# One 128-column matmul where both halves of a block list a chunk

## The chip, the cores and the metric

The kernel runs on one core of a Trainium2 chip. The metric is the device time of one execution in microseconds; the kernel before took 2024.06 us as the median of 7 runs (2017.86 to 2031.18). The engines are named as in the profile: PE is TensorE (PEld its weight loads), DVE is VectorE, ACT is ScalarE, POOL is GpSimd, and SP is the engine that only issues transfers.

## The reference

Two graph layers over 4096 nodes with 512 features. The adjacency matrix is sparse, some 32 neighbours a node, and given as a dense 4096 x 4096 array. Each layer normalizes its input first and adds its result to it.

```
h = max(layernorm(x), 0)
x = x + relu((d * adj * d^T) @ h @ W + b)            # layer 0
h = max(layernorm(x), 0)
e = leaky_relu(Wh1 + Wh2^T, 0.2)                     # layer 1, on h
att =  softmax(where(adj > 0,  e, -1e12))
neg = -softmax(where(adj > 0, -e, -1e12))
x = x + elu(concat(att @ h, neg @ h) @ wtrans)
```

## The kernel before

Layer 0 is computed densely on TensorE from the start to about 960 us. Beside it the kernel works out, for every pair of 64-row blocks of layer 1, which nodes its rows have as neighbours, sorted into lists of 128 places ("chunks"), so that layer 1 need not touch the rest.

Layer 1 (`sparse_layer1`) treats 64 blocks of 64 rows. Two blocks, numbered r = 2n and 2n + 1, form a pair n and share their gathered rows. For a pair POOL issues 21 indirect DMAs (`gather`, L506), one a chunk of 128 rows of 644 words, into three tiles: g0 with 8 chunks, g1 with 6 and a seventh that SP loads, the block's own rows, and g2 with 7. The even block r = 2n multiplies the chunks of g0 and g1, 15 of them, and the odd block those of g1 and g2, 14 of them. Each of the three tiles has two buffers, used by alternate pairs, so that the gathers of a pair can begin when the pair two places earlier has been read: those into g0 after its even product, those into g1 and g2 after its odd one. POOL runs them in this order: 8 gathers into g0, then 13 into g1 and g2, then 8 again. Which matmul they wait for is the last one that reads the tile's buffer.

A block's 64 rows are two halves of 32 rows. Each row has two weights for a neighbour, one for each softmax. The weights of a chunk are thus a tile of 128 columns, `p[:, k]`, ordered half, softmax, row: 64 columns for the first half and 64 for the second. A half does not have neighbours in every chunk. `HALVES` says which chunks each half needs, 10 of 15 in an even block and 11 of 14 in an odd one. `half_products` (L551) goes through both lists side by side: each step is two matmuls with 64 weight columns each, one writing rows 0 to 63 of the accumulator u and one writing rows 64 to 127, with different gathered rows streaming through each. An even block has 10 such steps, an odd one 11. In f32 each matmul appears as two weight loads and two matmul records.

The lists overlap. In even blocks both halves need chunks 3, 4, 10, 11 and 14, in odd ones 0, 1, 2, 3, 4, 6, 9 and 10. The kernel before multiplies these twice, once for each half, in different steps.

After a product (`product`, with the sums of the weights, cs, L580) ACT scales u into us (L1815). PE transposes us one block later (tp, L595), ACT copies the transposed values, and PE multiplies them by `wtrans` into o (`project1`, L1826): eight 128-column matmul records after every block. DVE and ACT finish o (L1843 to L1847) and SP stores it. The weights of the block two ahead (`weights`, L1765 to L1787) are made by ACT and DVE meanwhile. The order of instructions on each engine in layer 1 is set by a scheduler from the program's order; matmuls that are marked keep their place.

The loop over the blocks runs in this order for block k (abridged):

```
product(r)
if k + 4 - k % 2 < len(order):
    for a in ((0,), (1, 2))[k % 2]:
        gather1(order[k + 4 - k % 2] // 2, a)
if k + 2 < len(order):
    weights(order[k + 2])
if k:
    turn(order[k - 1])
```

The first pair is treated earlier (`product0`, L1541 for its sums), and two blocks have two more chunks that are multiplied apart (`late_h`).

Of the kernel before, what the change touches and what calls it, by code (L numbers as in the profile page):

```python
# [32 lines left out]
RB = 64  # L33
# [15 lines left out]
HALVES = (  # L49
    ((0, 1, 2, 3, 4, 10, 11, 12, 13, 14), (3, 4, 5, 6, 7, 8, 9, 10, 11, 14)),  # L50
    ((0, 1, 2, 3, 4, 6, 9, 10, 11, 12, 13), tuple(range(11))),
)
# [221 lines left out]
def gcn_gat_kernel(  # L274
# [26 lines left out]
    nc = tc.nc  # L301
# [36 lines left out]
    with sbuf(name="init", bufs=1) as init:  # L338
        column = init.tile([P, P], F32, name="column")
        nc.vector.memset(column[:, 0:1], 0.0)  # L340
        n = 1
# [60 lines left out]
    steps = [(c, r) for c in range(NK) for r in range(CAPS[c] // 8)]  # L402
# [148 lines left out]
    def half_products(r, u, p, row, chunks, end=True, pin=False, begin=True):  # L551


        for ks in zip(*chunks):
            for h, k in enumerate(ks):
                i = nc.tensor.matmul(  # L556
                    u[h * RB : (h + 1) * RB],
                    p[:, k, h].rearrange("p g i -> p (g i)"),
                    row(k),
                    start=begin and k == HALVES[r % 2][h][0],  # L560
                    stop=end and k == chunks[h][-1],
                )
                if pin:
                    tc.keep_in_program_order(i)

# [41 lines left out]
    with sbuf(name="y0", bufs=1) as y_pool, sbuf(name="wa", bufs=1) as wa_pool, sbuf(name="bits", bufs=4) as bits_pool, sbuf(name="small0", bufs=4) as small, ExitStack() as rest, ExitStack() as lists:  # L607
# [5 lines left out]
        def list_tables(pool):  # L613
            rank = pool.tile([P, EN], F32, name="rank")
            nc.gpsimd.iota(
                rank,
                [[-1, EN]],
                base=EN,
                channel_multiplier=0,
                allow_small_or_imprecise_dtypes=True,  # L620
            )
            before = pool.tile([P, NE + 1, NH], F32, name="before")
            start = pool.tile([NH, 1], F32, name="start")
            nc.gpsimd.iota(
                start,
                [[0, 1]],
                base=0,
                channel_multiplier=STR,
                allow_small_or_imprecise_dtypes=True,
            )  # L630
            return rank, before, start

        rank, before, start = list_tables(list_pool)
# [400 lines left out]
        def new_rows(pool, n):  # L1034
            rows = [pool.tile([P, ROW_W], F32, tag=f"h{k}", name=f"h{k}", bufs=1) for k in range(n)]
            for h in rows:
                nc.gpsimd.memset(h[:, ROW_T + 1 :], 0.0)
            return rows
# [94 lines left out]
        i0, n = GROUPS[0]  # L1133
# [362 lines left out]
        def early_pair(work, at_pool, prod, rows):  # L1496
# [63 lines left out]
            def product0(r):  # L1560
                u0[r] = bank(f"u{r}")

                def row(k):
                    gt, k0, n = parts0(r)[k >= parts0(r)[1][1]]
                    return gt[:, k - k0, :F].bitcast(F32)

                half_products(r, u0[r], ps0[r], row, HALVES[r % 2], False, r == blocks[0])

            def late_product0(r):
                def row(k):  # L1570
                    return late_h[:, k - slots0(r), :F]

                late = range(slots0(r), slots0(r) + n_late)
                half_products(r, u0[r], ps0[r], row, (late, late), begin=False)
                sum0(r, late)
# [77 lines left out]
        with sbuf(name="work0", bufs=2) as work, sbuf(name="rows0", bufs=1) as row_pool, sbuf(name="sums", bufs=3) as sum_pool, sbuf(name="at", bufs=6) as at_pool:  # L1653
# [4 lines left out]
            with tc.manual_schedule(engines=order - {engine.PE}):  # L1658
                rows = new_rows(row_pool, 3)
# [31 lines left out]
    def sparse_layer1():  # L1691
        nonlocal verdict
        with ExitStack() as pools:
# [105 lines left out]
            def product(r):  # L1799
                p, total = wgt.pop(r)  # L1800

                rl = None if r in first else inverse_sums(small, r, total)
                u = bank(f"u{r}")

                def row(k):
                    gt, k0, n = parts(r)[k >= parts(r)[1][1]]
                    return gt[:, k - k0, :F].bitcast(F32)

                half_products(r, u, p, row, HALVES[r % 2], r not in with_late)
                if r in with_late:  # L1810
                    ks = range(n_late)
                    half_products(r, u, lates.pop(r), lambda k: late_h[:, k, :F], (ks, ks), begin=False)
                rl = rl or inverse_sums(small, r, total)
                us[r] = work.tile([P, F], F32, tag="us", name=f"us{r}")
                nc.scalar.activation(us[r], u, AF.Copy, scale=rl)  # L1815
# [169 lines left out]
```

## Time and profile before

| what | us |
|---|---|
| median of 7 runs | 2024.06 |
| the profiled execution | 2027.42 |
| its span, first to last instruction | 2025.6 |
| PE busy | 1896.8 |
| L556 (u), 64-column matmul records x2604, busy | 624.4 |
| idle of PE just before L556 | 88.2 |
| L1826 (o), 128-column matmul records x496, busy | 230.9 |
| POOL gathers L506 x672, busy | 639.1 |
| mean granted TensorE clock | 0.974 |

The profiled execution lies 3.4 us above the median. Busy times of PE count overlapping records once. "Issue" as the cause of idle time means that the engine waited for nothing that the profile shows; "remote" means that a semaphore was raised by something that the profile can't name.

### The profile page before, as it was taken

The page shows a single profiled execution, that of the slowest core. Times are in us where ns is not written, and L with a number is a line of the kernel's source. Part 1 is how long each engine was busy: PE and PEld are TensorE (multiplying, and loading weights), DVE is VectorE, ACT ScalarE, POOL GpSimd, SP SyncE. Part 2 cuts the span into 40 slices and gives each one's busy share as a digit, 9 for nine tenths or more (in the row PEclk, how much of TensorE's full clock was granted, in tenths as well). Part 3 has the DMA queues.
Part 4 walks back from the last instruction along what each step waited for, and adds up shares of the span by engine and source line. Part 5 has one row for each costly group of instructions (what it writes and reads, how often), then busy time and mean ns, then how long its engine had stood idle before and what let it go on. Part 6 is the DMA issues. An engine that isn't in the chain of part 4 may idle for free.

```text
span 2025.6 us, 24509 instructions
## 1 busy us (share of the span) xinstructions
PE 1896.8 (94%) x7708; PEld 1056.3 (52%) x7708; DVE 1273.9 (63%) x2758; ACT 937.4 (46%) x2165; POOL 822.0 (41%) x919
## 2 busy tenths in 40 slices
PE   8999999999999999999779999999889898898988
PEld 3444468888888888884333333333333333333334
DVE  6766588898889979752625654646545555554552
ACT  6777733222213212221536654646555565564551
POOL 3110000033322233305536656666666666666640
PEclk9999999999999999999779989999999999998999
DMA  9999957576857676668857878788888787777850
GB/s 373 392 329 337 321 192 250 176 244 200 274 169 258 196 234 216 213 201 287 288 183 247 283 234 292 251 282 254 278 263 298 248 251 249 249 257 232 254 180 23
DMA packets 217218, 504.33 MB, mean 249 GB/s; under 512 B 35059, under 2 KB 69395, under 8 KB 217078
## 3 DMA queue, kind: packets, MB, share of 16 engines
q0 software_dynamic: 62560, 233.71, 35.8%
q1 hardware_dynamic: 114240, 236.49, 34.5%
q10 hardware_dynamic: 40278, 32.47, 5.1%
q8 instruction: 63, 1.03, 0.2%
q14 instruction: 77, 0.63, 0.1%
HBM read 457.77 MB, written 103.45 MB: 277 GB/s over the span
## 4 chain that ended last, share of the span: by engine, by line
PE 86%; issue 6%; DVE 2%; POOL 2%; ACT 1%; another core or an unknown queue 1%; DMA 1%; DVEq 0%; POOLq 0%; ACTq 0%
PE p L1105 30%; PE u L556 28%; PE o L1826 10%; PE acc L1064 5%; PE yp L890 5%; PE q L1465 3%; PE tp L595 2%; POOL g L506 2%; PE counts L867 1%; PE cs L1541 1%; PE tx L831 1%; DMA g<-table,idx 1%; DVE total L1787 0%; ACT z L1765 0%
## 5 line engine op out<-in xcount | busy, mean ns | idle before, releaser
L506 POOL DMA_INDIRECT g<-table,idx x672 | 639.1, 951 | 441.7 <-issue 176.1
L556 PE MATMUL u<-g,p 128*64 128x512 f32 x2604 | 624.4, 606 | 88.2 <-issue 76.7
L556 PEld LDWEIGHTS u<-g,p 128*64 128x64 f32 x2604 | 190.2, 138 | 460.5 <-issue 441.1
L442 POOL DMA_INDIRECT ld<-lst,off x160 | 144.0, 900 | 342.9 <-DMA ld<-lst,off 143.4
L1765 ACT ACTIVATE z<-s,g 128x64 f32<-128x64 f32 x812 | 259.5, 320 | 46.9 <-DMA g<-table 12.5
L1105 PE MATMUL p<-y,at 128*128 128x256 f32 x832 | 248.0, 380 | 0.7 <-issue 0.7
L1105 PE MATMUL p<-y,sums 128*128 128x256 f32 x832 | 247.4, 379 | 0.0
L1105 PE MATMUL p<-t,sums 128*128 128x256 f32 x832 | 245.3, 379 | 0.0
L1826 PE MATMUL o<-wt,ut 128*128 128x512 f32 x496 | 230.9, 610 | 1.8 <-DVE eo L1843 1.4
L1768 DVE TENSOR_TENSOR z<-z,y 128x512 f32<-128x512 f32 (+1 forms) x124 | 80.3, 648 | 209.7 <-ACT y L1767 109.1
L1787 DVE TENSOR_REDUCE total<-p 128x128 f32<-128x1920 f32 (+1 forms) x62 | 207.8, 3352 | 2.1
L1105 PEld LDWEIGHTS p<-y,at 128*128 128x128 f32 x832 | 157.1, 190 | 24.1 <-issue 3.2
L1105 PEld LDWEIGHTS p<-t,sums 128*128 128x128 f32 x832 | 158.0, 190 | 21.7 <-issue 0.2
L1105 PEld LDWEIGHTS p<-y,sums 128*128 128x128 f32 x832 | 158.0, 190 | 21.4
L1826 PEld LDWEIGHTS o<-wt,ut 128*128 128x128 f32 x496 | 93.4, 199 | 96.3 <-issue 94.6
L1777 DVE SCALAR_TENSOR_TENSOR p<-g,z 128x512 f32<-128x512 uint8 (+1 forms) x124 | 78.4, 632 | 103.1 <-ACT z L1773 86.5
L852 ACT ACTIVATE junk<-ar 128x1024 bf16<-128x1024 f32 x128 | 134.5, 1051 | 9.6 <-DMA ar<-in_adj 5.6
L930 ACT ACTIVATE m<-at 128x1024 uint8<-128x1024 f32 x110 | 113.0, 1047 | 53.4 <-DVE t_all L1032 14.4
L1773 ACT ACTIVATE e<-z 128x512 f32<-128x512 f32 (+1 forms) x124 | 67.1, 542 | 132.2 <-issue 79.2
L1777 DVE SCALAR_TENSOR_TENSOR p<-g,e 128x512 f32<-128x512 uint8 (+1 forms) x124 | 79.0, 637 | 74.3 <-ACT e L1773 26.0
L1105 PE MATMUL p<-t,at 128*128 128x256 f32 x416 | 123.9, 380 | 1.2 <-DVE w L975 1.2
L1064 PE MATMUL acc<-y,at 128*128 128x512 f32 x256 | 120.2, 594 | 0.0
(220 smaller groups left out, 2032.2 us busy)
## 6 DMA issues: line engine op xcount, KB each, us to landing
ar<-in_adj SPq DMA_DIRECT2D x128, 512.0 KB
at<-in_adj_t SPq DMA_DIRECT2D x112, 512.0 KB
table<-table SPq DMA_DIRECT2D x49, 1032.0 KB
table<-m ACTq DMA_DIRECT2D x48, 256.0 KB
g<-table,idx POOLq DMA_INDIRECT x672
g<-table SPq DMA_DIRECT2D x32, 322.0 KB
at<-in_adj_t SPq DMA_DIRECT2D x32, 256.0 KB
xr<-in_x SPq DMA_DIRECT2D x32, 256.0 KB
```

The costliest lines, as they stand in the source:

```text
L442: return nc.gpsimd.indirect_dma_start(out=lst_dram[g][e % TURNS][:, :], out_offset=bass.IndirectOffsetOnAxis(ap=off[g][:, e, c : c + 1], a ...
L506: i = nc.gpsimd.indirect_dma_start(out=gt[:, k, :], out_offset=None, in_=table[2 * n // RPT], in_offset=bass.IndirectOffsetOnAxis(ap=idx[n ...
L556: i = nc.tensor.matmul(u[h * RB : (h + 1) * RB], p[:, k, h].rearrange("p g i -> p (g i)"), row(k), start=begin and k == HALVES[r % 2][h][0 ...
L852: nc.scalar.activation(junk, ar, AF.Identity, accum_out=parts[j][:, c : c + 1])
L890: nc.tensor.matmul(yp, hx_t[j][:, c * P : (c + 1) * P], w0_sb[:, c, :], start=c == 0, stop=c == FC - 1,)
L930: nc.scalar.activation(m, at, AF.Sign)
L1064: nc.tensor.matmul(a, at[:, 0, it * P : (it + 1) * P], y0[j], start=j == 0, stop=j == NJ - 1)
L1105: i = nc.tensor.matmul(out, left[:, x * P : (x + 1) * P], right, start=jp == 0 and first, stop=jp == NP - 1 and (final or not first),)
L1765: nc.scalar.activation(z[:, c], s, AF.Identity, bias=t[:, c])
L1777: nc.vector.scalar_tensor_tensor(p[:, k : k + n, :, g], mask.rearrange(four, h=2), 0.0, x.rearrange(four, h=2), ALU.is_gt, ALU.mult,)
L1787: nc.vector.tensor_reduce(total, q, AX.X, ALU.add)
L1826: i = nc.tensor.matmul(halves[j], uts[j][:, g, c, :], wts[g][:, c, :], start=g == 0 and c == 0, stop=g == 1 and c == FC - 1,)
```

## The change

In `half_products`, chunks that stand in both halves' lists are taken out of the lists. They are multiplied first, each by one matmul with all 128 columns of `p[:, k]`, into all 128 rows of u. What is left of the two lists, five chunks a half in an even block and three in an odd one, then follows in pairs of 64 columns as before. The accumulation begins with the first step and ends with the last.

```diff
-        for ks in zip(*chunks):
-            for h, k in enumerate(ks):
-                i = nc.tensor.matmul(
-                    u[h * RB : (h + 1) * RB],
-                    p[:, k, h].rearrange("p g i -> p (g i)"),
-                    row(k),
-                    start=begin and k == HALVES[r % 2][h][0],
-                    stop=end and k == chunks[h][-1],
-                )
+        both = [k for k in chunks[0] if k in chunks[1]]
+        alone = zip(*[[k for k in ks if k not in both] for ks in chunks])
+        steps = [(k, k) for k in both] + list(alone)
+        for n, (k0, k1) in enumerate(steps):
+            start, stop = begin and n == 0, end and n + 1 == len(steps)
+            if k0 == k1:
+                halves = [(u, p[:, k0].rearrange("p h g i -> p (h g i)"), k0)]
+            else:
+                halves = [
+                    (u[h * RB : (h + 1) * RB], p[:, k, h].rearrange("p g i -> p (g i)"), k)
+                    for h, k in enumerate((k0, k1))
+                ]
+            for rows, left, k in halves:
+                i = nc.tensor.matmul(rows, left, row(k), start=start, stop=stop)
```

An even block now has the steps 3, 4, 10, 11, 14 and then (0, 5), (1, 6), (2, 7), (12, 8), (13, 9); an odd one 0, 1, 2, 3, 4, 6, 9, 10 and then (11, 5), (12, 7), (13, 8). The last step that reads g0 (chunks 0 to 7 of an even block) is the eighth where it was the fifth; the last that reads g1 in an odd block (chunks 0 to 6) is the ninth where it was the seventh. Line numbers below the function grow by 5.

## The prediction

> **What bounds the kernel now.** I read the page first, for engine shares and the chain.
>
> ```profile
> PE 1896.8 (94%) x7708; PEld 1056.3 (52%) x7708; DVE 1273.9 (63%) x2758; ACT 937.4 (46%) x2165; POOL 822.0 (41%) x919
> PE 86%; issue 6%; DVE 2%; POOL 2%; ACT 1%; another core or an unknown queue 1%; DMA 1%; DVEq 0%; POOLq 0%; ACTq 0%
> L556 PE MATMUL u<-g,p 128*64 128x512 f32 x2604 | 624.4, 606 | 88.2 <-issue 76.7
> L1826 PE MATMUL o<-wt,ut 128*128 128x512 f32 x496 | 230.9, 610 | 1.8 <-DVE eo L1843 1.4
> ```
>
> TensorE carries the chain, and the line that changes, L556, is 28% of it. But L556 also has 76.7 us of idle time put down to "issue", a wait for nothing that the profile shows, while L1826 has almost none. The list of waits says how it is spread, and that POOL has a twin of it:
>
> ```profile
> POOL g L506 <- remote: 81.5, 27, 3.2
> POOL g L506 <- PE u L556: 80.8, 25, 12.5
> PE u L556 <- issue: 76.7, 63, 3.0
> ```
>
> Then the timeline of PE and of POOL over one pair of blocks. Each f32 matmul is two records, so an odd block (11 steps) is 44 and an even one (10 steps) 40.
>
> ```profile
> 1399.36 9.66 PE L556 MATMUL u<-g,p 128*64 128x512 f32 x44
> 1408.96 0.66 PE L595 MATMUL tp<-ident,us 128*128 128x128 f32 x4
> 1409.45 3.60 PE L1826 MATMUL o<-wt,ut 128*128 128x512 f32 x8
> 1412.88 0.28 PE L580 MATMUL cs<-ones,total 128*128 128x1 f32 x2
> 1413.09 7.94 PE L556 MATMUL u<-g,p 128*64 128x512 f32 x34
> 1423.02 0.59 PE L556 MATMUL u<-g,p 128*64 128x512 f32 x1 [1.99 <-issue]
> 1424.44 2.72 PE L556 MATMUL u<-g,p 128*64 128x512 f32 x5 [0.83 <-issue]
> ...
> 1431.20 0.28 PE L580 MATMUL cs<-ones,total 128*128 128x1 f32 x2
> 1431.40 1.08 PE L556 MATMUL u<-g,p 128*64 128x512 f32 x4
> ```
>
> ```profile
> 1405.88 0.94 POOL L506 DMA_INDIRECT g<-table,idx  x1 [4.59 <-PE u L556]
> ...
> 1420.88 0.95 POOL L506 DMA_INDIRECT g<-table,idx  x1 [0.30 <-issue]
> 1424.86 0.95 POOL L506 DMA_INDIRECT g<-table,idx  x1 [3.04 <-remote]
> ```
>
> The odd product runs without a gap; the even one stops near its end, and so does nearly every even product. POOL issues 13 gathers (1405.88 to 1421.82), then waits 3.04 us. By the program's order its next gather, into g0, waits for the tenth matmul of the even product. That one ended at 1417.6 by its record, but the trace's semaphore events have its increments at 1424.558 and 1424.600. So PE's increments are held back. Over the 28 runs of 13 gathers this increment comes 18.6 to 18.9 us after the run's first gather, and increments due from about 7.2 us on come late, in steps of about 0.7 us. In the hold PE still passes 57 to 70 instructions (weight loads and matmul records; median 61.5 counted from 7.2 us; two runs 79 and 82), then one per 0.7 us until the hold ends. The median slow part lasts 4.7 us. No view names what holds them; that PE's budget is counted in instructions is my inference. Two things speak for it. Between 1001 and 1014 us L1541's matmuls, which increment nothing, crawl at the same 0.7 us. And in the pair below the even product began late, so that L1826 (4 instructions per 0.86 us, not 8) filled more of the hold:
>
> ```profile
> 1092.11 3.70 PE L1826 MATMUL o<-wt,ut 128*128 128x512 f32 x8 [1.35 <-DVE eo L1843]
> 1095.86 8.59 PE L556 MATMUL u<-g,p 128*64 128x512 f32 x37
> 1105.30 1.09 PE L556 MATMUL u<-g,p 128*64 128x512 f32 x3 [0.86 <-issue]
> ```
>
> There 37 records passed, not 34, and the slow part was 2.1 us.
>
> **The change, part by part.** *Array time.* 44 records of pairs take 9.60 us to the next line's start, 0.86 a step; eight records of L1826, four 128-column matmuls, take 3.43, also 0.86. Even blocks share 5 chunks and keep 5 pairs, odd share 8 and keep 3: 10 and 11 steps, as before. So array time is 0 changed. This is the main trap: two 64-column matmuls already run side by side. Weight loads, two of 190 ns in place of four of 138, lie under 0.43 us records: 0, with that cover everywhere.
>
> *Instructions.* A shared step has 4, not 8. Even: 80 to 60; odd: 88 to 56.
>
> *The hold, one pair, t=0 at the odd product's start.* Before: 9.60 + tp 0.49 + o 3.43 + cs 0.21 puts the even product at 13.7, and 8.6 + 4.1 more make 26.4 without idle. Starts from 1080.28 to 1680.68 hold 19 pairs, 31.6 each, so 5.2 are lost. Of these the crawl takes 4.7 minus 6 instructions' work (0.65), 4.0; half-clock stretches after it (granted clock 0.96 to 0.98) and short waits take the rest.
> After: two releases move. Gathers into g1 wait for the last odd step that reads g1: step 7 before, step 9 now. So POOL's run begins 1.7 later, 8.1 instead of 6.4; the hold is 15.3 to 26.8 instead of 13.6 to 25.1. The g0 release moves from even step 5 to step 8 (t=20.6): still inside, so the 8 gathers into g0 start at 27.1, 1.7 later. SP's load of the own chunk waits for the same g1 release; a few SP transfers swap places with it, and both are needed a pair later: 0. POOL's order, ACT's and DVE's are unchanged.
> PE in the new hold: shared steps until 18.0 (2.7 us, 13 instructions), 5 pair steps to 22.3 (40), tp to 22.8 (8): 61. Net of one leaving per 0.7 us the old budget is 61.5 - 6.9/0.7 = 52 (48 to 69), the new count at 22.8 is 50, and L1826 adds 3.2 a us: PE slows at 23.4, inside o. To 26.8 that is 3.4 us, in which 5 instructions (1.05 us of o's work) pass: 2.35 lost instead of 4.0. Gain 1.65, times 28 pairs: 46 us.
> Bounds: at 48 it slows at 22.6 and loses 4.15 - 0.9, a gain of 0.75 a pair (21 us); at 69 it never slows, and POOL is next: 13 gathers 15.95 + gap 3.03 + 8 gathers 9.69 + 0.30 = 29.0 a pair, a gain of at most 2.6 (73 us). I take 46; most counts are 48 to 58 net.
>
> *The switch inside a product.* No row shows a 512-wide 128-column matmul followed by 64-column ones. Nearest: pair to tp starts 0.52 apart where 0.43 is usual, 0.09 more; each product has two such changes before and after. Bounds: 0 (the cs switch does it already) to 0.21 (a record's 0.59 must drain, less 0.43, plus 0.05 on the first record's 643 ns). I take 0.05, near the 0.09: 62 products, 3 us. [...]
>
> *Increments.* The last four 64-column matmuls of each product now increment one by one: 6 in an even product instead of 3, 5 in an odd instead of 2. The two increments above stand 42 ns apart; 3 x 42 ns x 62 is 8 us at most, and none below, but all but the last fall under the next step: I take 0. [...]
>
> *Start of layer 1.* PE crawls in L1541 too, to 1014.6, set by POOL; fewer instructions ahead of it are worth 0 to 3 us. I take 0.
>
> *What is next.* ACT's us of the even block comes at 27 instead of 27.8, and its transposes a product later; DVE's eo already cost o 1.35 us once. I count neither.
>
> Sum: 46 - 3 = 43 less. The profiled execution took 2027.42 (span 2025.6), 3.4 above the median 2024.06 of seven (2017.86 to 2031.18): 1984, and against the median **1981**. The profiled time lies in the band of the others, so I take it that the crawl is in all of them.
>
> **Rivals.** *A, no change.* The budget is time, not instructions: PE stops 7 us after the hold begins. Then run, hold and crawl move together 1.7 later and the loss stays: 2024. For it: most crawls start at 13.4 to 15.0 of the run. Against it: the pair at 1095.
> *B, slower.* A is true and the switch inside a product costs its 0.21: 62 x 0.21 = 13, so 2037. It decides once the crawl shrinks by less than 0.46 us a pair. For it: pairs and 128-column work never follow each other at full width now. Against it: the 0.09 at tp.
> *C, POOL bound.* No crawl, 29.0 a pair: 2024 - 73 = 1951. Against it: held gathers still follow PE's release.
> That the 128-column matmuls aren't made is excluded by the program's order.
>
> **The numbers.** My forecast 0.60 (1960 to 2006), C 0.08, A 0.12, B 0.20. This kernel's times spread so that some 0.3% can be told from no change. Faster 0.68, same 0.12, slower 0.20. Range 1949 to 2032: C's end to most of B; about 0.2 is left out.
>
> **What will show it.** L556's records fall from 2604 to some 1800 (128-column 806, 64-column 992) with about 0.43 us a step record; POOL's g L506 <- remote gap stays near 3.0; its runs start later after the odd product's start; "issue" before PE moves from u to o or tp and shrinks to about 45 us; pairs of about 30.0 us. Wrong if the odd or even product grows beyond 9.6 and 8.6 us where nothing stops it, or the idle at "issue" keeps its 77 us.

## The result, and the profile after

The changed kernel takes 2003.74 us (median of 13 runs, 1990.05 to 2018.25) beside 2025.60 us for the kernel before (34 runs). The ratio is 0.9891, with a 95% interval of 0.9869 to 0.9913: 22 us or 1.1% faster. The forecast was 43 us, 1981. The direction was right and the forecast gain was twice too large.

Its profiled execution took 2014.11 us (span 2012.3, mean granted clock 0.970), 10 us above its own median, so the two profiles differ by 13 us and not by 22. From the page of the changed kernel: engine shares, chain, the groups of u and o, and below them the waits of POOL and PE.

```profile
PE 1901.9 (95%) x6860; PEld 1086.3 (54%) x6860; DVE 1273.4 (63%) x2758; ACT 937.6 (47%) x2165; POOL 822.4 (41%) x919
PE 71%; issue 9%; POOL 8%; DVE 4%; DMA 2%; another core or an unknown queue 2%; ACT 2%; POOLq 0%; DVEq 0%; ACTq 0%
L567 PE MATMUL u<-g,p 128*128 128x512 f32 (+1 forms) x1798 | 636.9, 621 | 53.9 <-issue 49.4
L1831 PE MATMUL o<-wt,ut 128*128 128x512 f32 x496 | 231.7, 609 | 10.9 <-DVE rl L590 4.4
```

```profile
POOL g L506 <- PE u L567: 79.2, 20, 9.1
POOL g L506 <- remote: 65.4, 23, 3.6
PE u L567 <- issue: 49.4, 55, 5.1
```

Idle time before u fell from 88.2 to 53.9 us (-34.3); idle time before o rose from 1.8 to 10.9 (+9.1); and u itself is busy 636.9 us instead of 624.4 (+12.5; on a chip where nothing stops PE it is +9.0, from 574.1 to 583.1). These three make -12.7 of the 13.3 us between the spans. The chain no longer stays with PE: POOL's share went from 2% to 8%. Waits of POOL's gathers for something unnamed came down from 27 to 23 although the program's runs of 8 and 13 gathers are the same: some runs no longer end where they did. The timeline shows that, first PE and then POOL, over one stretch of the changed kernel (start, length, engine, line, tiles, number of records, and in brackets the idle time before):

```profile
1291.74 0.66 PE L600 MATMUL tp<-ident,us 128*128 128x128 f32 x4
1292.23 3.60 PE L1831 MATMUL o<-wt,ut 128*128 128x512 f32 x8
1295.81 6.93 PE L567 MATMUL u<-g,p 128*128 128x512 f32 x15
1303.55 0.59 PE L567 MATMUL u<-g,p 128*128 128x512 f32 x1 [0.81 <-issue]
1304.95 0.59 PE L567 MATMUL u<-g,p 128*64 128x512 f32 x1 [0.81 <-issue]
1306.38 1.01 PE L567 MATMUL u<-g,p 128*64 128x512 f32 x1 [0.84 <-issue]
1308.51 1.01 PE L567 MATMUL u<-g,p 128*64 128x512 f32 x1 [1.11 <-issue]
1309.93 3.72 PE L567 MATMUL u<-g,p 128*64 128x512 f32 x9 [0.41 <-issue]
```

```profile
1284.35 0.95 POOL L506 DMA_INDIRECT g<-table,idx  x1 [0.30 <-issue]
1288.42 0.94 POOL L506 DMA_INDIRECT g<-table,idx  x1 [3.12 <-remote]
1289.66 0.95 POOL L506 DMA_INDIRECT g<-table,idx  x1 [0.30 <-issue]
...
1305.93 0.95 POOL L506 DMA_INDIRECT g<-table,idx  x1 [0.30 <-issue]
1311.22 0.94 POOL L506 DMA_INDIRECT g<-table,idx  x1 [4.34 <-PE u L567]
```

POOL starts at 1288.42 and gathers 15 times without a break until 1306.88: the 7 gathers of g2 and, right behind them, the 8 of the next g0. PE crawls from 1301 on, in an odd product. Before, all gaps inside the products (78.0 us in all) were in even ones; now 29.7 us are in odd ones and 19.1 in even ones. Over the whole trace the strict alternation of 13 and 8 is gone: from 1075 us on there are 17 runs of 13, 11 of 14, 6 of 15, 11 of 8, 5 of 7 (a break under 0.8 us does not end a run here). To size the crawl, take every step between successive starts on PE, weight loads and matmuls alike, that is longer than 0.62 us, less a usual 0.21, from each run's start to 4 us after its end. The sum is 133.8 us before and 113.8 us after. Six runs of 15 have 42.6 us of the latter (5.8 to 7.6 each), and two runs of 13 that began only 1.3 to 1.4 us after the gathers ahead of them have 15.5. The other 15 runs of 13 have 21.3 together, 1.4 each, where a run of 13 before had 3.9. The runs of 14 have 1.0 each, so the length alone does not make the crawl. In the runs of 15 PE passes only 22 to 34 instructions, counted from 7.2 us as in the prediction, before it crawls; in the kernel before the median was 61.5. Pairs of blocks took 31.4 us each before and 30.9 after on the mean, but they are no longer alike: 27 to 28 us, then 34 to 38.

The clock follows the crawl. In each of the six runs of 15 the records grant PE half its clock for 6.8 to 10.2 us, from 4 to 6 us after the crawl has begun; two of the records above last 1.01 us instead of 0.59. From 1060 us on PE has half its clock for 61 us before and for 87 us after.

### The profile page after: what moved, and what is told of

Its sections match the earlier page's. It is cut to its first block, busy times and chain, and to the rows that moved or that the text cites. A ratio compares the mean times of both kernels' runs of the same rounds, so it can differ in the third digit from the quotient of the medians.

```text
span 2012.3 us, 22814 instructions
## 1 busy us (share of the span) xinstructions
PE 1901.9 (95%) x6860; PEld 1086.3 (54%) x6860; DVE 1273.4 (63%) x2758; ACT 937.6 (47%) x2165; POOL 822.4 (41%) x919
## 4 chain that ended last, share of the span: by engine, by line
PE 71%; issue 9%; POOL 8%; DVE 4%; DMA 2%; another core or an unknown queue 2%; ACT 2%; POOLq 0%; DVEq 0%; ACTq 0%
PE p L1110 27%; PE u L567 20%; POOL g L506 8%; PE o L1831 7%; PE acc L1069 5%; PE yp L895 5%; PE q L1470 3%; DMA g<-table,idx 1%; PE tp L600 1%; ACT z L1770 1%; PE counts L872 1%; DVE key L429 1%; DVE lst L427 1%; DMA ld<-lst,off 1%
## 5 line engine op out<-in xcount | busy, mean ns | idle before, releaser
L567 PE MATMUL u<-g,p 128*128 128x512 f32 (+1 forms) x1798 | 636.9, 621 | 53.9 <-issue 49.4
L567 PEld LDWEIGHTS u<-g,p 128*128 128x128 f32 (+1 forms) x1798 | 226.7, 164 | 406.8 <-issue 387.4
L1831 PE MATMUL o<-wt,ut 128*128 128x512 f32 x496 | 231.7, 609 | 10.9 <-DVE rl L590 4.4
L895 PE MATMUL yp<-w_sb,hx_t 128*128 128x512 f32 x256 | 119.0, 608 | 0.0
```

Source lines behind the costliest of these rows:

```text
L567: i = nc.tensor.matmul(rows, left, row(k), start=start, stop=stop)
L895: nc.tensor.matmul(yp, hx_t[j][:, c * P : (c + 1) * P], w0_sb[:, c, :], start=c == 0, stop=c == FC - 1,)
L1831: i = nc.tensor.matmul(halves[j], uts[j][:, g, c, :], wts[g][:, c, :], start=g == 0 and c == 0, stop=g == 1 and c == FC - 1,)
```

## The experiments

Times are given beside the kernel before on the same chip, since chips turned out to differ. On some the kernel before takes 2000 to 2026 us, as above, and its profile has the idle time at "issue"; on four others it takes 1860 us, and has none. "Held" and "free" stand for these two below.

**Undoing one half at a time.** `early_release` keeps the instructions and undoes the later releases, and `two_of_64` keeps the order and undoes the 128-column matmuls. `mixed` has the changed kernel's releases with many more changes of shape, `pause_after` breaks POOL's run. A single number in the lists of steps is a shared chunk; edits are abridged, here and below.

```diff
 early_release:
+            steps = ([3, 4, (0, 5), (1, 6), (2, 7), (12, 8), (13, 9), 10, 11, 14],
+                     [0, 1, 2, 3, 4, 6, (11, 5), (12, 7), (13, 8), 9, 10])[r % 2]
 mixed:
+            steps = ([3, (0, 5), 4, (1, 6), 10, (12, 8), 11, (2, 7), 14, (13, 9)],
+                     [0, (12, 7), 1, (13, 8), 2, 3, 4, 6, (11, 5), 9, 10])[r % 2]
 two_of_64:
-            if k0 == k1:
+            if k0 == k1 and len(steps) < 10:
 pause_after (in gather1, ahead of the gathers):
+                for _ in range(4 if a == 2 else 0):
+                    tc.keep_in_program_order(nc.gpsimd.memset(holes[1408], 0.0))
```

> The same steps as in the changed kernel, five and three pairs, but ordered so that the last matmul that reads g0 is the fifth of the even product and the last that reads g1 the seventh of the odd one, as before the change. Theory 1 (the gain is that fewer instructions have to pass while PE's increments are held): the gain stays, and as POOL's 13 gathers begin at 6.4 us after the odd product's start, as before, the runs of 13 and 8 should no longer merge into runs of 14 and 15; the crawl is then about 2 us a pair and the time 1980 to 1995. Theory 2 (the gain is the later release): 2024 plus some 10 us for the switches, 2030 to 2040.

> The changed kernel's order of steps, but each shared chunk is multiplied by two matmuls of 64 columns, as before the change: the instructions of before (80 and 88 a product), the release of after, no 128-column records in u and so no switch inside a product. Theory 1 (instructions): the crawl is back at about 4 us a pair, 2015 to 2030. Theory 2 (the later release alone): as the changed kernel or better by what its switches cost, 1990 to 2004. If products without a stall take 9.6 and 8.6 us again, the longer products of the changed kernel come from the mix of 128 and 64 columns.

> The changed kernel's steps with the same releases (eighth step of the even product, ninth of the odd one), but pairs and shared chunks alternate: 15 switches between 128 and 64 columns inside the two products of a pair instead of 2. If a switch costs what a product without a stall has grown by (0.17 to 0.2 us), products grow by 2.2 to 2.6 us a pair, of which what falls under the hold is hidden: 2035 to 2070. If a switch costs my 0.05: 2010 to 2025. If it costs nothing: 2004.

> The changed kernel with four small memsets on POOL (some 0.4 us each, 1.6 us together) between the gathers into g1 and those into g2, so that no 13 gathers follow each other without a break. If the hold begins some 7 us after the start of an unbroken run of gathers, it comes later or not at all, the crawl falls under 1 us a pair and the time is set by POOL, 28 pairs of about 29 to 30.5 us: 1970 to 2000. If the hold goes with the number of gathers and not with the break, all of it ends 1.6 us later and up to 28 x 1.6 = 45 us are added: 2030 to 2050.

All four fell on a free chip, where the kernel before took 1860.27 us: early_release 1869.07 (1.0044, 1.0030 to 1.0058), two_of_64 1862.78 (1.0017, 1.0005 to 1.0028), mixed 1924.33 (1.0357, 1.0340 to 1.0374), pause_after 1888.98 (1.0163, 1.0146 to 1.0180). They say nothing of the hold, but there is no better place to price the change of shape, because nothing stops a product. From the start of a product to that of the transposes, odd and even, in us: 9.59 and 8.74 in two_of_64, 9.87 and 9.01 in early_release, 10.57 and 10.31 in mixed. So 64 columns alone take what they took before, in the new order too; the mix is what lengthens products.

**The two kernels themselves on a free chip.**

> The changed kernel itself, on the chip of this set of runs. In the runs of early_release, two_of_64, mixed and pause_after PE's increments were not held back at all and the kernel before took 1860 us. Theory 1 (the whole gain is in the hold): where there is no hold, nothing is gained, and the longer products (0.17 to 0.2 us each) cost 0 to 12 us: 1860 to 1872. Theory 2 (the gain is the later release): some 20 us are gained without the hold too, 1840. Where the increments are held in these runs: about 22 us under the kernel before.

> The kernel before, for its trace on the chip of this set of runs. If the hold is what separates 2024 us from 1860 us, a run of 1860 us shows no line of L556 with idle time at issue, 'POOL g L506 <- remote' near 0, and pairs of about 26.4 us, which is 5.2 us less for each of 31 pairs, 161 us; layer 0 should take as long as before. If layer 0 or the product itself is faster, the difference lies elsewhere.

The changed kernel took 1869.90 us beside 1860.81: 1.0048 (1.0027 to 1.0070), so there it is slower. The kernel before, profiled at 1866.77 us, shows on its page:

```profile
PE 1836.4 (98%) x7708; PEld 1040.8 (56%) x7708; DVE 1274.3 (68%) x2758; ACT 936.4 (50%) x2165; POOL 827.2 (44%) x919
L556 PE MATMUL u<-g,p 128*64 128x512 f32 x2604 | 574.1, 596 | 0.0
L1826 PE MATMUL o<-wt,ut 128*128 128x512 f32 x496 | 226.9, 601 | 11.3 <-DVE rl L585 9.4
```

The idle time before u is 0.0 where it was 88.2 us, and half the clock is granted for 12 us from 1060 us on, where it was 61. The last part of layer 0 (L1465) begins at 908.4 us, where it was 909.9; the third product of layer 1 at 1033.6 instead of 1065.7, and from there to the last product's start 59 products take 799 us instead of 927, 27.1 a pair instead of 31.4. So nearly all of the 160 us between the chips lie in layer 1, and go with the hold. POOL runs up to 244 gathers without a break of 0.8 us in two_of_64 on the free chip, and PE has no idle time at "issue" before u, tp or o. The hold is therefore no property of a run of gathers as such, which is what the prediction took it for.

One odd block of each kernel on the free chip, of the kernel before first: product, transposes, o, sums, and the next product.

```profile
1404.88 9.66 PE L556 MATMUL u<-g,p 128*64 128x512 f32 x44
1414.47 0.66 PE L595 MATMUL tp<-ident,us 128*128 128x128 f32 x4
1414.97 3.60 PE L1826 MATMUL o<-wt,ut 128*128 128x512 f32 x8
1418.40 0.28 PE L580 MATMUL cs<-ones,total 128*128 128x1 f32 x2
1418.61 6.66 PE L556 MATMUL u<-g,p 128*64 128x512 f32 x30
```

```profile
1403.46 9.84 PE L567 MATMUL u<-g,p 128*128 128x512 f32 x28
1413.23 0.66 PE L600 MATMUL tp<-ident,us 128*128 128x128 f32 x4
1413.72 3.60 PE L1831 MATMUL o<-wt,ut 128*128 128x512 f32 x8
1417.16 0.28 PE L585 MATMUL cs<-ones,total 128*128 128x1 f32 x2
1417.30 8.12 PE L567 MATMUL u<-g,p 128*128 128x512 f32 x26
```

Start to start, the product grew from 9.59 to 9.77 (+0.18), and the step from the sums to the product, which no longer changes shape, shrank from 0.21 to 0.14 (-0.07). A block is 0.11 us longer (13.73 to 13.84), and 62 of them make 7 us of the 9 measured. In mixed, where blocks are longer by 0.85 (odd; 10.57 + 0.43 + 3.44 + 0.14) and by 1.51 (even, worked out with the same other steps), 31 pairs make 73 us of the 64 measured.

**The other order, and more instructions.** `pairs_first` is the changed kernel with the pairs ahead, and `filler_before` the kernel before with 24 more instructions in the even product.

```diff
 pairs_first:
+            steps = ([(12, 8), (13, 9), (0, 5), (1, 6), (2, 7), 3, 4, 10, 11, 14],
+                     [(11, 5), (12, 7), (13, 8), 0, 1, 2, 3, 4, 6, 9, 10])[r % 2]
 filler_before:
+            for _ in range(3 if more is not None and n == 3 else 0):
+                for h, k in enumerate(ks):
+                    nc.tensor.matmul(more[h * RB : (h + 1) * RB, 1:2],
+                                     p[:, k, h].rearrange("p g i -> p (g i)"),
+                                     ones[:, 0:1], start=True, stop=True)
```

> The changed kernel's steps with the pairs ahead of the shared chunks, so that a product goes from 64 to 128 columns inside and ends with 128, as the transposes after it do (even: 12/8, 13/9, 0/5, 1/6, 2/7, then 3, 4, 10, 11, 14; odd: 11/5, 12/7, 13/8, then 0, 1, 2, 3, 4, 6, 9, 10). Theory of the switch: from the products without a stall so far, there and back costs (10.57 - 9.87) / 2 = 0.35 us and a product that ends with 128 columns saves 0.07 at the transposes, so a product takes about 9.69 and 8.83 us here, +0.10 where the changed kernel has +0.18; where nothing is held that is 0 to 6 us over the kernel before. If what costs is the first record after any change of shape, whatever its direction, products take 9.77 and 8.91 again and the time is that of the changed kernel, some 9 us over.

> The kernel before with six more matmuls of 64 columns and one streamed column in every even product, between its third and fourth step (they write a column that nothing reads): 24 more instructions. Where PE's increments are held in these runs: if PE may pass a number of instructions, 24 / 9.3 a us = 2.6 us are lost a pair, 2.6 x 28 = 72 us; if it may pass a time, only what the matmuls themselves take, 0.1 to 0.25 us each, 17 to 42 us. Where nothing is held: the even product is longer by 0.6 to 1.5 us, and the time 10 to 45 us over the kernel before, less what POOL's own pace of 26.5 us a pair hides.

Both were on a held chip (kernel before 2025.91 us). pairs_first took 2053.67 us, 1.0141 (1.0115 to 1.0167). Its products without a stall take 9.70 and 8.84 us, as worked out ahead (9.69 and 8.83), so the prices of a change of shape, taken from the other kernels, hold here too. It has eight runs of 21 gathers, and this is one of them:

```profile
1967.72 3.60 PE L1834 MATMUL o<-wt,ut 128*128 128x512 f32 x8
1971.36 4.50 PE L570 MATMUL u<-g,p 128*64 128x512 f32 x18
1977.38 0.59 PE L570 MATMUL u<-g,p 128*64 128x512 f32 x1 [1.51 <-issue]
1979.48 0.59 PE L570 MATMUL u<-g,p 128*64 128x512 f32 x1 [1.52 <-issue]
1982.98 1.01 PE L570 MATMUL u<-g,p 128*128 128x512 f32 x1 [2.91 <-issue]
1985.78 1.01 PE L570 MATMUL u<-g,p 128*128 128x512 f32 x1 [1.79 <-issue]
1987.91 4.53 PE L570 MATMUL u<-g,p 128*128 128x512 f32 x7 [1.12 <-issue]
```

POOL gathers from 1957.99 to 1983.93 without a break, PE crawls from 1975 to 1987, and the sum defined above is 9.8 to 11.3 us for each of the eight, 85.5 of the kernel's 171.7 us. From 1336 us on its runs of 13 that stand alone have 0.0. Here the number of instructions is the usual one, 70 to 81 from 7.2 us on, and it is the length of the run that makes the crawl long.

filler_before took 2119.39 us, 93 more than the kernel before (one run, so a few us either way). In the one even product at the end that nothing stops, the filler adds 0.36 us (9.09 instead of 8.73), 11 us in all.

```profile
1727.36 2.79 PE L565 MATMUL u<-g,p 128*64 128x512 f32 x12
1729.98 0.47 PE L557 MATMUL cs<-ones,p 128*64 128x1 f32 x12
1730.30 2.77 PE L565 MATMUL u<-g,p 128*64 128x512 f32 x11
1733.74 0.59 PE L565 MATMUL u<-g,p 128*64 128x512 f32 x1 [0.67 <-issue]
1736.54 0.59 PE L565 MATMUL u<-g,p 128*64 128x512 f32 x1 [2.21 <-issue]
1737.94 6.05 PE L565 MATMUL u<-g,p 128*64 128x512 f32 x15 [0.81 <-issue]
```

The even product stops after 23 of its records, where it used to stop after 34. Counted from 7.2 us of a run of 13, PE passes 67 instructions (median) before it crawls, and comes to the crawl at about 12 us; in the kernel before it was 61.5 instructions and 14 us. In runs of 13 the number stays and the time moves: there it is instructions that are rationed. Rival A's budget in time would have cost the fillers' own time alone, 11 us by this product and 17 to 42 by the expectation. The 93 us are also more than the 72 forecast for a number; half the clock is granted for 145 us from 1060 us on, where it was 61. The number is not the same in all runs, though: in the changed kernel's runs of 15 it is 22 to 34, and there the crawl begins 11.8 to 13.7 us after the run's start, which a budget in time would fit better.

**One parity at a time, and fewer bytes.** `even_64` and `odd_64` undo the 128-column matmuls in one kind of block. `short_rows` reads 516 words of each row instead of 644; it leaves out the masks and mixes the rows, so only its time means something.

```diff
 even_64 (odd_64 with r % 2 == 0):
-            if k0 == k1:
+            if k0 == k1 and (len(steps) < 10 or r % 2 == 1):
 short_rows:
-                out=gt[:, k, :], in_=table[2 * n // RPT],
+                out=gt[:, k, :516], in_=packed(table[2 * n // RPT], 516),
-                    mask = gt[:, :, ROW_W:].bitcast(U8)[...]
+                    mask = gt[:, :, : ROW - ROW_W].bitcast(U8)[...]
```

> The changed kernel's order in both products, but in even blocks every shared chunk is two matmuls of 64 columns again (80 instructions in the even product, 56 in the odd). Where PE's increments are held: the even product is the one that lies in the hold, so if instructions are what is rationed, the crawl comes back and the time is 2015 to 2035, at or over the kernel before; if it is the later release that gained, it is the changed kernel less 30 x 0.18 = 5 us, 1995 to 2000. Where nothing is held: half the cost of the mix, some 4 us over the kernel before.

> The counterpart: in odd blocks every shared chunk is two matmuls of 64 columns (88 instructions in the odd product, 60 in the even). Where PE's increments are held: if only what lies in the hold counts, this gains as the changed kernel does, less the odd product's own 0.18 us, 1990 to 2005; and as PE reaches the release of g1 no sooner, POOL's runs merge no more often. If instructions are rationed in the odd product too (the merged runs of 14 and 15 gathers reach into it), 2005 to 2020. Where nothing is held: some 4 us over the kernel before.

> The kernel before, but each gather of layer 1 reads 516 words a row instead of 644, from a packed view of the same table, so that rows and masks are not the right ones; the number of gathers, of instructions and of waits is unchanged. Where PE's increments are held: if the hold comes from the transfers falling behind POOL (queue 0's engines are busy until 2 us after the last gather), 20% fewer bytes let them keep up, the hold shrinks or goes and the time falls towards the 1860 us of the chip without it; if it comes from the gathers as such, their number or POOL's work on them, nothing changes, 2020 to 2030. Where nothing is held: 1855 to 1862.

A free chip again (kernel before 1861.22 us): even_64 1.0026 (1.0011 to 1.0042), odd_64 1.0035 (1.0020 to 1.0051), where the whole change costs 1.0048; short_rows 1854.45 us in one run. What they were made for stays open.

**The halves once more, where increments are held.** two_of_64_held and short_rows_held are the kernels above, run again.

> The kernel of two_of_64 once more, for a chip on which PE's increments are held (the first time they were not: 1.0017). If instructions are rationed, the later release alone gains nothing: 2015 to 2035, beside a kernel before of 2026. If the later release is what gained, 1990 to 2004. On a chip without the hold: 1862 again.

> The kernel of short_rows once more, for a chip on which PE's increments are held: gathers of 516 words a row where there were 644, wrong rows and masks. If the transfers that fall behind POOL make the hold, it shrinks or goes, 1860 to 1980; if the gathers as such do, 2020 to 2030. On a chip without the hold: 1854 again.

Held chip, kernel before 2018.08 us. short_rows_held took 2019.17 us in one run: with 20% fewer bytes nothing changes. Its hold ends 2.6 to 3.0 us after the last gather, as in the kernel before (2.7 to 3.0; in each kernel one run has 4.1 to 4.2), and PE passes 65 instructions before it crawls. So the hold does not shrink with the bytes. The number of gathers was the same, so that it goes with their number was not tried.

two_of_64_held took 2045.40 us, 1.0145 (1.0106 to 1.0185). The changed kernel's order without its fewer instructions loses 1.5%. Waits and groups show where:

```profile
PE tp L600 <- issue: 61.9, 49, 2.6
PE u L567 <- issue: 20.6, 11, 7.3
```

```profile
L567 PE MATMUL u<-g,p 128*64 128x512 f32 x2604 | 577.0, 596 | 11.4 <-issue 11.4
L1831 PE MATMUL o<-wt,ut 128*128 128x512 f32 x496 | 278.2, 711 | 21.8 <-issue 16.8
```

The runs stay at 13 and 8, and the crawl has moved on, 64 instructions after the hold's start, from the end of the even product into tp and o. The even product takes its clean time, 8.73 to 8.81 us, in 26 of 31 cases, and o has become 47 us longer. In the clock records PE is granted half its clock for 140 us from 1060 us on, where it was 61 us before; that the move into tp and o causes this was not tried.

**Fewer instructions with the old releases, and breaks.**

> The kernel of early_release once more, for a chip on which PE's increments are held: the changed kernel's instructions, but the releases of g0 and g1 at the steps of before (fifth and seventh). two_of_64_held showed that the later releases without the fewer instructions cost 1.5%. If that cost is in the changed kernel too and comes from where the hold falls on PE's work, the releases of before with the fewer instructions take 1970 to 1990, beside a kernel before of 2018 to 2026, and the runs of gathers stay at 8 and 13. If PE, no longer stopped, reaches the releases before POOL has finished, the runs merge into 21 as they did in pairs_first, the crawl in a merged run is about 11 us, and the time is 2020 to 2055. On a chip without the hold: 1.0044 of the kernel before again.

> The kernel before with four small memsets on POOL between the gathers into g1 and those into g2, which in pause_after made a break of 2.1 us where 0.3 is usual. Where PE's increments are held: if the hold begins 7.2 us after the start of an unbroken run of gathers, a run of 13 becomes one of 6 and one of 7, no increment is late by more than a few us, and the crawl (4.0 us a pair in the kernel before) falls under 1 us; the pair is then set by POOL, 29.0 + 1.8 = 30.8 us where the kernel before takes 31.4, 2000 to 2015. If a break of 2.1 us does not end the hold, it ends 1.8 us later than before, 28 x 1.8 = 50 us are added, 2060 to 2080. Where nothing is held: as pause_after, 1.5% over the kernel before.

These two fell on a free chip: early_release 1.0022 (1.0012 to 1.0032), and pause_before, which is the kernel before with the same memsets, 1.0150 (1.0133 to 1.0167).

> The kernel of early_release a third time, as both runs so far fell on chips where nothing is held. Where PE's increments are held: 1970 to 1990 if the later releases are what cost the changed kernel its lost half and the runs of gathers stay at 8 and 13; 2020 to 2055 if PE, no longer stopped, lets the runs merge into 21, with some 11 us of crawl in each. On a chip without the hold: 1.002 to 1.005 of the kernel before again.

This time the increments were held: 1986.23 us beside 2001.85, 0.9930 (0.9905 to 0.9955). It is faster, but by 0.7% where the first theory had 1.4 to 2.8%, and not slower as the second had it. (Its 1986 us lies in the first theory's range only because the kernel before took 2002 us here, and 2018 us on the same chip some ten minutes earlier; a time means something only beside its own set.) Its page:

```profile
L570 PE MATMUL u<-g,p 128*128 128x512 f32 x1798 | 636.3, 615 | 37.2 <-issue 34.3
L1834 PE MATMUL o<-wt,ut 128*128 128x512 f32 x496 | 228.5, 602 | 18.2 <-issue 11.9
```

Its runs merge as the changed kernel's do, with the old releases: 17 of 13, 9 of 14, 10 of 15, one of 21. The runs of 15 have 43.6 of its 92.8 us of slow time, and PE passes 34 to 56 instructions in them before it crawls. So merging does not need the later release. That it comes from a PE that is no longer stopped fits all traces: on held chips runs merge in the kernels with fewer instructions and stay at 13 and 8 in those with the old number or more, and on free chips they merge with the old number too. No run tried it by itself.

> The changed kernel with four small memsets on POOL (2.1 us between two gathers in pause_after) between the 8 gathers into g0 and the 13 that follow them, so that the two runs cannot merge. Where PE's increments are held: if the merged runs are what costs the changed kernel its lost half, the runs are 8 and 13 throughout, the crawl of 7 to 8 us that comes with every third pair is gone, and what remains is POOL's own 9.7 + 2.1 + 15.95 + 3.0 = 30.75 us a pair, 1995 to 2010 beside a kernel before of 2025, as gathers then set the pace. If crawls of that size come with runs of 13 too, the time is 2020 to 2050. Where nothing is held: POOL has 21 x 1.25 + 2.1 = 28.3 us a pair, 1.5% over the kernel before as in pause_after.

> The kernel of pause_before once more, for a chip on which PE's increments are held: a break of 2.1 us between the gathers into g1 and those into g2. If the hold begins 7.2 us after the start of an unbroken run of gathers, the crawl falls under 1 us a pair and the time is 2000 to 2015 beside a kernel before of 2018 to 2026. If such a break does not end the hold, it ends 1.8 us later than before, 28 x 1.8 = 50 us are added, 2050 to 2080. Where nothing is held: 1.5% over the kernel before again.

A free chip for both: break_after 1.0255 (1.0237 to 1.0274), 1% more than expected, and pause_before again 1.0136 (1.0118 to 1.0155). Whether a break in POOL's gathers ends the hold, and whether keeping the runs apart would give the rest of the gain, was not seen.

## Why the direction was right and the forecast gain twice too large

*Instructions are rationed in the hold.* Right for runs of 13, by filler_before, and the records fell as forecast, 2604 to 1798. two_of_64_held shows the same from the other side: with the old number of instructions the new order gains nothing. That the budget is one number for every run, 61.5, did not hold: in runs of 15 it is about half of it.

*The hold, one pair: loss 2.35 instead of 4.0, gain 1.65 times 28.* This is the step that failed, in its "times 28". The pair worked out exists: where a run of 13 keeps its distance in the trace of after, the slow time is 1.4 us instead of 3.9, even better than forecast. But the sum took the pattern of 13 and 8 as given, and with it POOL's 29.0 us as a limit "next" that lay beyond the forecast's 30.0. A PE without the crawl needs 27 to 28 us, reaches the next release before POOL has finished, and POOL runs on. The runs are then often 13, 14 and 15 long in turn, and in those of 15 PE passes 22 to 34 instructions where the median before was 61.5, so that the crawl comes back with 6 to 8 us, in the odd product. Why the number is smaller there stays open, and break_after, made to keep the runs apart, fell on a free chip. Rival C named POOL's 29.0 us as a floor; what was missing is that coming near it changes the runs. The profiled gain in idle time around u and o is 34.3 - 9.1 = 25 us instead of 46. The sum also left the half clock as it was, and it grew from 61 to 87 us; 26 us more at half the clock are worth up to 13 us, an estimate. Two releases of the kernel before came later than the 18.6 to 18.9 us read in the prediction, at 19.1 and 20.1 us; the sum does not hang on them.

*The later release.* Counted as part of the gain through the hold's place. By the same sum, the order alone would change nothing (the same 4.0 us). It measured +1.5% alone (two_of_64_held), fewer instructions alone -0.7% (early_release_third), both together -1.1%, each beside the kernel before of its own set. They do not add, and the sum had no term for where the crawl falls.

*The switch inside a product, 0.05 us, 0 to 0.21.* Sized too low, within its bounds: a product grew by 0.18, the step from the sums lost 0.07, 0.11 a block, 7 us instead of 3. There and back inside a product is 0.35 us (mixed against early_release, (10.57 - 9.87) / 2). Each change costs here, and the argument from an unchanged number of changes did not hold: beside the narrow sums a change costs 0.07, between two 512-wide matmuls about 0.18. That a record's 0.59 must drain, the premise of the upper bound, was the author's estimate and is not shown: in 54 of 60 products of the profile after, the first 64-column record starts 0.52 us after the last 128-column one, where 0.43 is usual.

*Increments, 0.* Nothing contradicts it: pairs_first came out at 9.70 and 8.84 us with the changes of shape alone reckoned. *Start of layer 1, 0.* The third product started at 1067.8 us instead of 1065.7, and PE's idle time at "issue" in the sums of the first pair is 18.5 us instead of 15.5. It gained nothing.

*What was said to show it.* "Issue" before PE's u was to fall to about 45 us and is 49.4; it was to move to o or tp, and went to the odd product instead; o and tp have 5.5 us of it. Pairs were to take 30.0 us and take 30.9. POOL's gap was to stay near 3.0 us: 65.4 / 23 = 2.8.

Against the median: -46 and +3 were forecast, and 7 us of switches with -22 in all leave -29 for the hold.

## What to carry to other kernels

Taking a stall from one engine can change the rhythm of the engine that feeds it. Work out the pair after the change for both engines, and ask what the feeder does when its release comes early: here it ran on, in runs of 14 and 15 gathers where there were 13, and the stall came back in those of 15, 5.8 to 7.6 us each. And before tuning against a stall that no view can name, look at the same kernel on another chip: here the sign of the change depends on it, 1.1% faster where increments are held and 0.5% slower where they are not.

## What the hardware did that was not expected

The hold goes with the chip as far as seen: the same program took 2002 to 2026 us or 1860 us. Two chips were measured twice; one was free both times, the other held both times. It goes along with what the traces hold. The part of the page that lists transfers has a median time to landing on free chips and none on held ones, here for the kernel before on the first chip and on a free one:

```profile
g<-table,idx POOLq DMA_INDIRECT x672
```

```profile
g<-table,idx POOLq DMA_INDIRECT x672, 5.1
```

Every trace from a held chip has 16,800 to 18,600 records of raised semaphores, and every one from a free chip 29,600 to 30,100; what is missing is missing from layer 1's gathers above all. In runs of 13 the hold lets some 60 to 70 instructions pass, is the same with 20% fewer bytes, and ends 2.6 to 3.0 us after the last gather. Whether recording an execution has a part in the hold was not tried: each timed execution has its span and clock recorded, and none ran without. If it has, the 1.1% is a gain for recorded executions on such chips only, and the 0.5% loss is what the change does to the kernel itself. That stays open.
